# Attention scores and projections in plain fp32 on row tiles of the array, with pairs of PSUM banks

## The chip, the cores and the metric

The kernel runs on one core of a Trainium2 chip. The metric is the device time of one execution in microseconds (us). A core has a tensor engine (PE, which writes its results to the eight banks of PSUM), VectorE (DVE), ScalarE (ACT), GpSimd (POOL), a queue of DMA issues (SP) and 16 DMA engines. Every engine runs its instructions in the order in which the program issues them.

## What is computed

Eight batches of 512 tokens with 256 channels go through two layers. Each layer is an attention block and a feed-forward block, each added to its input, each behind a layer norm. Cut to what matters here:

```
def L0_attention(x, ctx):                 # x [8, 512, 256], ctx [8, 512, 128]; 16 heads of depth 16
    q, k, v = heads(x @ Wq + bq), heads(x @ Wk + bk), heads(x @ Wv + bv)
    att = where(causal, (q @ k.T) / 4, -inf)
    y = softmax(att) @ v
    qc, kc, vc = heads(x @ Wcq + bcq), heads(ctx @ Wck + bck), heads(ctx @ Wcv + bcv)
    y = y + softmax((qc @ kc.T) / 4) @ vc
    return y @ Wp + bp
def L1_attention(x, ctx):
    q, k, v = heads(x @ Wq + bq), heads(ctx @ Wk + bk), heads(ctx @ Wv + bv)
    return (softmax((q @ k.T) / 4) @ v) @ Wo + bo
x = x + L0_attention(layernorm(x), ctx)
x = x + L0_ffn(layernorm(x))              # weights and activations quantised
x = x + L1_attention(layernorm(x), ctx)
x = x + L1_ffn(layernorm(x))              # 8-bit steps with one scale per tensor
```

All inputs and outputs are fp32. The feed-forwards round to integers, so the attention in front of them has to be close to fp32.

## The kernel before

Attention is cut into units (kind, batch): S is the causal self attention, C the cross attention of layer 0, X that of layer 1. There are 8 of each, 24 in all, in the order `UNITS`: S and C of batches 0 to 5, then X units among the rest, and X units alone at the end. A unit has four groups of four heads, 96 groups in all.

**Operands.** A value is split in two float32r parts (a rounded form of fp32), its rounded high part and the rest; a product of two values is then three products of parts. The input of a projection is split so (`ln_job`, `ctx_job`), its weights too (`load_weight`; the parts are kept in DRAM and loaded again at each use). `prep_job` projects queries and keys of half of the heads, six matmuls per weight with 256 inputs and three with 128 (line 446), adds the bias on ScalarE (line 452) and splits the result on GpSimd (lines 238 and 255). `stack_job` copies the parts by DMA (lines 481 and 485) into the stack of a group, one of `NQK` = 4: 124 rows, so that one matmul over all of them gives the three products of parts, with zeros in K where another head's rows lie.

**Scores.** They are computed twice. `max_one` computes 128 queries of one head against up to 512 keys, one matmul into one bank (line 555), and VectorE takes the row maxima (line 565; for S with the causal mask added, line 560). `rows_job` negates the 16 columns of maxima (lines 576 and 577), turns them on PE (line 584) and writes them by DMA as four further rows of the stack, with ones in K, so that the second computation subtracts the maximum by itself. `exp_one` computes transposed scores, 128 keys against up to 512 queries, into one bank (line 627), adds the mask for S with a bf16 matmul (line 641), and ScalarE takes the exponential into a tile p (line 643). `av_part` multiplies by V in plain fp32, four heads side by side, each in its own 32 columns of the array (line 670); a column of ones in V gives the sums.

**After them.** `evac_job` copies the outputs to DRAM, `post_job` loads the sums, inverts them, loads them back spread over the heads' rows, multiplies (line 727) and splits again. `outproj_job` projects by `proj_tokens` (line 505, used for V too) and adds the residual. `last_heads_job` and `last_proj_job` do the same for the last unit in smaller pieces (lines 798, 813, 843, 852).

**The order of the work.** A planner (`Plan`) holds a rough clock for each engine. Jobs are generators that wait for due times on the tensor engine's clock; the main stream picks an output part first, then a step of maxima or one of exponentials, keeping the maxima `LEAD` steps ahead; work of jobs for PE gets its turn after the main stream had a share (`SHARE`). The program's order follows from these clocks, and on the chip each engine keeps to it. `CAPS` limits the PSUM banks: three for maxima, three for exponentials, two for outputs, three for work beside, out of eight.

**The end.** Behind the attention, the last feed-forward runs alone (from about 1495 us on); it is not changed.

## Time and profile before

| | |
|---|---|
| three runs | 1597.45, 1597.27, 1595.65 us; median 1597.27 |
| the profiled execution, span of its instructions | 1596.5 us |
| busy: PE, DVE, ACT, POOL | 94%, 81%, 68%, 52% |
| mean granted tensor clock | 0.981 |
| score matmuls, lines 555 and 627 | 1536 each |
| output matmuls, line 670 | 3072 records (two for each fp32 matmul) |
| row maxima, line 565 (128 x 512) | 1024 of 680 ns |
| exponentials, line 643 (128 x 512) | 1344 of 603 ns |
| bytes moved by DMA | 244.17 MB |

The profile page gives the busy time of each engine, groups of instructions by line, and the chain of work that ended last, followed back through what released each step. A matmul's length in it holds the drain of the array, which overlaps the next matmul; the distance between starts is what a stream of them costs. A stretch is a window of time with the busy time of each engine in it.

### The profile page before, as it was taken

The numbers are of one execution on the slowest core, as the hardware profiler recorded it, in microseconds if no ns is written. First come the engines' busy times: TensorE is split into PE (matmuls) and PEld (weight loads), VectorE is DVE, ScalarE is ACT, GpSimd is POOL, SyncE is SP. The second block draws the span as 40 slices with busy tenths as digits, with TensorE's granted clock in tenths as the row PEclk, the third lists the DMA queues.
The fourth block names the chain that finished last, engine by engine and source line by source line (L and its number), as shares of the span: only waits on it lengthen the run. The fifth ranks groups of instructions, "written<-read, shape, count | busy, mean of one in ns | idle before, by whom it ended". The sixth has DMA issues, their size and how long they took to land.

```text
span 1596.5 us, 28434 instructions
## 1 busy us (share of the span) xinstructions
PE 1500.6 (94%) x8911; PEld 905.9 (57%) x8928; DVE 1300.4 (81%) x3038; ACT 1087.0 (68%) x1934; POOL 832.8 (52%) x1059
## 2 busy tenths in 40 slices
PE   4989999999999999999999999999999989999876
PEld 3755665655665656655566465655555546555435
DVE  6878687887888888898869987888898768786687
ACT  3547667577676777677666767767776756777694
POOL 6543452653636745669447626456657434432328
PEclk8999999999999999999999999999999999999989
DMA  4664645755666646756467545755556564553422
GB/s 134 198 176 125 172 126 131 188 144 153 174 174 182 175 113 172 179 159 171 122 163 189 151 118 157 194 139 144 146 150 180 136 198 139 155 155 103 159 68 106
DMA packets 186110, 244.17 MB, mean 153 GB/s; under 512 B 82776, under 2 KB 92248, under 8 KB 185448
## 3 DMA queue, kind: packets, MB, share of 16 engines
q1 hardware_dynamic: 185960, 242.36, 56.6%
q8 instruction: 71, 1.16, 0.3%
q14 instruction: 79, 0.65, 0.1%
HBM read 101.18 MB, written 52.15 MB: 96 GB/s over the span
## 4 chain that ended last, share of the span: by engine, by line
PE 73%; DVE 11%; DMA 5%; ACT 4%; POOL 2%; issue 2%; SPq 1%; DVEq 0%; ACTq 0%; POOLq 0%
PE bank L670 18%; PE bank L555 18%; PE bank L627 17%; PE bank L446 6%; PE bank L505 5%; DVE mx L565 3%; ACT g L1414 2%; DMA qk<-qkt 2%; DVE bank L560 2%; PE bank L1063 2%; PE bank L641 2%; PE bank L381 2%; PE bank L1000 1%; DVE mhl L576 1%; ACT p L643 1%
## 5 line engine op out<-in xcount | busy, mean ns | idle before, releaser
L643 ACT ACTIVATE p<-bank 128x512 f32<-128x512 f32 x1344 | 737.5, 603 | 342.0 <-PE bank L627 221.9
L565 DVE TENSOR_REDUCE mx<-bank 128x1 f32<-128x512 f32 x1024 | 649.1, 680 | 120.7 <-PE bank L555 117.1
L555 PE MATMUL bank<-qk 124*128 124x512 f32 (+3 forms) x1536 | 552.4, 396 | 16.8 <-DMA scrz<-zr 7.3
L627 PE MATMUL bank<-qk 128*128 128x512 f32 (+3 forms) x1536 | 525.3, 387 | 11.9 <-DMA qk<-mrow 4.6
L555 PEld LDWEIGHTS bank<-qk 124*128 124x128 f32 x1536 | 283.7, 192 | 149.6 <-issue 69.6
L670 PE MATMUL bank<-p,v 128*32 128x512 f32 (+3 forms) x3072 | 365.4, 554 | 0.3
L627 PEld LDWEIGHTS bank<-qk 128*128 128x128 f32 x1536 | 282.2, 191 | 119.9 <-issue 42.2
L560 DVE CUSTOM_DVE_ANT_0 bank<-bank,mask 128x128 f32<-128x128 f32 (+3 forms) x512 | 238.4, 517 | 74.2 <-PE bank L555 71.9
L238 POOL TENSOR_SCALAR qkt<-qkt 128x512 fp32r<-128x512 f32 x92 | 57.0, 620 | 214.9 <-ACT qkt L452 145.2
L670 PEld LDWEIGHTS bank<-p,v 128*32 128x32 f32 x3072 | 66.6, 108 | 109.2 <-issue 81.3
L255 POOL TENSOR_TENSOR qkt<-qkt 128x512 fp32r<-128x512 f32 x92 | 118.3, 1286 | 7.7
L452 ACT ACTIVATE qkt<-bank,qk_bias 128x512 f32<-128x512 f32 x96 | 66.2, 689 | 37.0 <-PE bank L446 27.0
L641 PE MATMUL bank<-ident_b,mask_b 128*128 128x256 bf16 (+1 forms) x320 | 83.9, 262 | 0.0
L560 DVE DVE_READ_ACCUMULATOR2_ANT mx<- 128x1 f32 x512 | 71.9, 140 | 0.0
L727 POOL TENSOR_TENSOR oc<-oc,rb 128x512 f32<-128x512 f32 x31 | 39.7, 1282 | 60.7 <-DMA rb<-scrz 51.5
L243 ACT COPY ev<-bank 128x512 f32<-128x512 f32 x81 | 47.3, 583 | 19.8 <-PE bank L670 15.7
L1004 DVE SCALAR_TENSOR_TENSOR h<-bank,so,bc_l_b 128x512 f32<-128x512 f32 x64 | 47.2, 740 | 8.2 <-PE bank L1000 5.3
L641 PEld LDWEIGHTS <-mask_b 128*128 128x128 bf16 x320 | 30.7, 96 | 36.4 <-issue 26.2
L1482 PE MATMUL bank<-w2q,gq 128*128 128x256 bf16 x256 | 33.5, 295 | 13.2 <-POOL gq L259 6.5
L1414 ACT ACTIVATE g<-bank,b1s,sc_x 128x512 f32<-128x512 f32 x64 | 43.0, 971 | 2.5 <-POOL y L1396 2.5
L1413 PE MATMUL bank<-tyt,w1q 128*128 128x512 bf16 x127 | 37.6, 387 | 7.5 <-DVE tyt L1393 3.2
L761 POOL TENSOR_TENSOR xb<-xb,bc_l_bp 128x256 f32<-128x256 f32 x32 | 23.2, 739 | 38.9 <-DMA xb<-in_x 38.9
(264 smaller groups left out, 2059.8 us busy)
## 6 DMA issues: line engine op xcount, KB each, us to landing
qk<-qkt SPq DMA_DIRECT2D x288, 128.0 KB
qk<-qkt SPq DMA_DIRECT2D x576, 64.0 KB
scro<-ev SPq DMA_DIRECT2D x94, 256.0 KB
oc<-scro SPq DMA_DIRECT2D x47, 256.0 KB
rb<-scrz SPq DMA_DIRECT2D x47, 256.0 KB
x_d<-xb SPq DMA_DIRECT2D x15, 512.0 KB
xa_s<-in_x SPq DMA_DIRECT2D x8, 512.0 KB
xb<-in_x SPq DMA_DIRECT2D x8, 512.0 KB
```

What stands on the lines that cost most here:

```text
L255: nc.gpsimd.tensor_tensor(dst, full, high.bitcast(F32), ALU.subtract)
L446: nc.tensor.matmul(ps, wv[:, a, k, :], xs[:, e, k, :], start=(j == 0), stop=(j == len(seq) - 1))
L452: nc.scalar.activation(full, ps, AF.Identity, bias=bias)
L505: nc.tensor.matmul(ps[:, (t - t0) * C : (t - t0 + 1) * C], lhs[:, a, k, t * P : (t + 1) * P], wv[:, e, k, :], start=(j == 0), stop=(j == l ...
L555: nc.tensor.matmul(ps[:, :n], q[:, qt * P : (qt + 1) * P], k[:, :n], start=True, stop=True)
L560: nc.vector.tensor_tensor_reduce(out=ps[:, :n], in0=ps[:, :n], in1=mask[:, T - n :], scale=1.0, scalar=-3.0e38, op0=ALU.add, op1=ALU.max, ...
L565: nc.vector.tensor_reduce(dst, ps, AX.X, ALU.max)
L627: nc.tensor.matmul(ps[:, off : off + n], k[:, kt * P : (kt + 1) * P], q[:, q0:], start=off == 0, stop=kind != "S",)
L641: nc.tensor.matmul(diag, mask_b, ident_b.unsqueeze(1).broadcast_to([P, n, P]), start=False, stop=True)
L643: nc.scalar.activation(p, ps, AF.Exp, scale=0.25)
L670: nc.tensor.matmul(banks[av_t[G]][32 * j : 32 * j + 32, T - n :], v_t[un % 2][:, kt, h * VST : h * VST + 32], p, start=(i == 0), stop=last,)
L1414: nc.scalar.activation(g[:, f, b, :], ps, AF.Gelu, scale=sx[:, 2:3], bias=b1s[:, f : f + 1])
```

## The change

Scores, projections and their operands are plain fp32, with no split anywhere.

A group's operands are one tile of 128 rows, [row, (Q, K), 512], and there are six such tiles (`NQK` = 6). Each head has 32 rows, which is one row tile of the array: row 0 is for minus the maximum (ones in K, through the bias), rows 1 to 16 are the depth, the rest zeros. `prep_job` projects one group: weights are spread on the chip, once, to this layout (`spread`, in `weights_job`, which keeps all of them in SBUF), and the evacuation with the bias writes the operands directly. There is no `stack_job`.

A step of `max_one` or `exp_one` now covers two heads: one matmul for each, on two of the four row tiles, into the two banks of a pair. One reduction with negation (VectorE) or one exponential (ScalarE) then reads both banks. For S, steps of several sizes are packed, and both the maxima and the exponentials get their mask from bf16 matmuls on the whole array. Three pairs serve both uses; the last two banks are for outputs and for the work beside, one each (`CAPS`, `zone`).

The outputs stay in SBUF: sums go by DMA to a small tile, their inverses through DRAM into a tile of the outputs' layout, and GpSimd multiplies group by group. The output projection contracts four blocks of 128 rows (32 for each head, of which 16 carry values). The planner books a plain fp32 matmul of T columns as `2 * T` columns at 2400 per us (before: `4 * T`), a switch of the array's tiling with 0.08 us, and two lanes of row tiles that run side by side.

```diff
-NQK = 4  # operand stacks of four heads that are alive at once
-LEAD = 38  # steps that the maxima run ahead of the exponentials
+NQK = 6
+LEAD = 2.5
...
+MAXS = {"X": [(p, (qt,)) for qt in range(NT) for p in (1, 0)]}
+MAXS["S"] = [(p, qts) for qts in ((0, 2), (1,), (3,)) for p in (1, 0)]
+EXPS = {"X": [(p, (kt,)) for kt in range(NT) for p in (0, 1)]}
+EXPS["S"] = [(p, kts) for kts in ((0,), (1, 3), (2,)) for p in (0, 1)]
+AVS = {"X": [(0, 1), (2, 3)], "S": [(0,), (1, 2, 3)]}
...
-CAPS = {"sm": 3, "st": 3, "av": 2, "gn": 3}
+CAPS = {"sm": 2, "st": 2, "av": 1, "gn": 1}
+SWITCH = 0.08
...
-    def pe(self, cols, *deps):
-        return self.run("pe", 0.003 + cols / 2400, *deps)
+    def _pe_start(self, mode, *deps):
+        t = max(self.now, *(d + LAT for d in deps), 0.0)
+        if mode != self.mode:
+            t = max(t, *self.lane) + SWITCH
+            self.mode = mode
+        return t
+
+    def pe(self, cols, *deps, mode="full"):
+        t = max(self._pe_start(mode, *deps), *self.lane) + 0.003 + cols / 2400
+        self.clock["pe"] = t
+        self.lane = [t, t]
+        return t
+
+    def pe_rows(self, p, cols, *deps):
+
+        t = max(self._pe_start("rows", *deps), self.lane[p])
+        self.clock["pe"] = t + 0.02
+        self.lane[p] = t + cols / 2400 + 0.01
+        return self.lane[p] + 0.1
...
-    banks = [psum.tile([P, 512], F32, name=f"bank{i}") for i in range(8)]
+    pairs = [psum.tile([P, 2, T], F32, name=f"pair{i}") for i in range(4)]
+    banks = [pairs[i // 2][:, i % 2] for i in range(8)]
...
-    qk_t = [wp.tile([P, 3, 2, T], F32R, name=f"qk{i}") for i in range(NQK)]
+    qk_t = [wp.tile([P, 2, T], F32, name=f"qk{i}") for i in range(NQK)]
...
+    def spread(nm, u, raw, eng):
+
+        nk = WT[nm].shape[1]
+        for k in range(nk):
+            for h2 in range(2):
+                dst = WT[nm][:, k, 2 * u : 2 * u + 2].rearrange("p g (h c e) -> p g h c e", h=2, c=2)
+                src = raw[:, k * P : (k + 1) * P].rearrange("p (g c d h) -> p g h c d", g=2, c=2, h=2)
+                eng.tensor_copy(dst[:, :, h2, :, 1 : D + 1], src[:, :, h2])
...
-            seq = [(a, e, k) for a, e in PARTS for k in range(nk)]
-            for j, (a, e, k) in enumerate(seq):
-                if j % 2 == 0:
-                    yield pe_next()
-                nc.tensor.matmul(ps, wv[:, a, k, :], xs[:, e, k, :], start=(j == 0), stop=(j == len(seq) - 1))
-                tm = plan.pe(T)
...
+            for k in range(nk):
+                yield pe_next()
+                nc.tensor.matmul(ps, WT[nm][:, k, g], xs[:, k, :], start=(k == 0), stop=(k == nk - 1))
+                tm = plan.pe(2 * T)
             used(key, ring, tm)
...
+            t = evacuate(qk_t[G % NQK][:, i], ps, T, tm, bias=bias_of(nm, g))
...
-        ps = banks[pb]
-        nc.tensor.matmul(ps[:, :n], q[:, qt * P : (qt + 1) * P], k[:, :n], start=True, stop=True)
-        t = plan.pe(n)
...
+        ps = pairs[pb // 2]
+        size = [(qt + 1) * P if kind == "S" else T for qt in qts]
+        offs = [sum(size[:n]) for n in range(len(qts))]
+        for off, n, qt in zip(offs, size, qts):
+            for c in range(2):
+                rows = slice(32 * (2 * p + c), 32 * (2 * p + c) + 32)
+                q, k = qk_t[G % NQK][rows, 0], qk_t[G % NQK][rows, 1]
+                nc.tensor.matmul(
+                    ps[:, c, off : off + n], q[:, qt * P : (qt + 1) * P], k[:, :n],
+                    start=off == 0, stop=kind != "S",
+                )
+        t = plan.pe_rows(p, 2 * sum(size))
         if kind == "S":
-            nc.vector.tensor_tensor_reduce(
-                out=ps[:, :n], in0=ps[:, :n], in1=mask[:, T - n :], scale=1.0, scalar=-3.0e38,
-                op0=ALU.add, op1=ALU.max, accum_out=dst,
+
+            first, n = size[0] // P - 1, len(qts)
+            step = size[-1] // P if n == 2 else 1
+            for c in range(2):
+                diag = ps[:, c].rearrange("p (a b) -> p a b", b=P)[:, first : first + (n - 1) * step + 1 : step]
+                nc.tensor.matmul(diag, ident_b, mask_b.unsqueeze(1).broadcast_to([P, n, P]), start=False, stop=True)
+            t = plan.pe(2 * n * P)
+        for off, n, qt in zip(offs, size, qts):
+            nc.vector.tensor_reduce(
+                mx_t[G][:, 2 * p : 2 * p + 2, qt], ps[:, :, off : off + n], AX.X, ALU.max, negate=True
             )
-        else:
-            nc.vector.tensor_reduce(dst, ps, AX.X, ALU.max)
-        t = op("dve", n, t)
+            t = op("dve", 2 * n, t)
...
+            for c in range(2):
+                j = 2 * p + c
+                rows = slice(32 * j, 32 * j + 32)
+                q, k = qk_t[G % NQK][rows, 0], qk_t[G % NQK][rows, 1]
+                nc.tensor.matmul(
+                    ps[:, c, off : off + n], k[:, kt * P : (kt + 1) * P], q[:, q0:],
+                    start=off == 0, stop=kind != "S",
+                )
+                p_t[G, kt, j] = pt[:, c, off : off + n]
             off += n
...
+        t = plan.pe_rows(p, 2 * off)
...
+        nc.scalar.activation(pt[:, :, :off], ps[:, :, :off], AF.Exp, scale=0.25)
...
-            t = plan.pe(4 * n + 150)
+            t = plan.pe(2 * n + 60, mode="cols")
...
-                    acc[t // 2][0][:, (t % 2) * C : (t % 2 + 1) * C], yt[:, a, u, t * P : (t + 1) * P], wv[:, e, u, :],
-                    start=False, stop=(u, a) == (1, 1) and t % 2 == 1,
+                    acc[t // 2][0][:, (t % 2) * C : (t % 2 + 1) * C], y[:, g, t * P : (t + 1) * P], WT["Wo"][:, g],
+                    start=False, stop=g == 3 and t % 2 == 1,
```

## The prediction

> **What bounds the kernel now.** I read the page first (busy shares, the chain that ended last), then the stretches, then the tensor engine's own timeline, because a busy share alone does not say whether an engine streams or only has something in flight.
>
> ```profile
> PE 1500.6 (94%) x8911; PEld 905.9 (57%) x8928; DVE 1300.4 (81%) x3038; ACT 1087.0 (68%) x1934; POOL 832.8 (52%) x1059
> ...
> PE 73%; DVE 11%; DMA 5%; ACT 4%; POOL 2%; issue 2%; SPq 1%; DVEq 0%; ACTq 0%; POOLq 0%
> ```
>
> ```profile
> 100.00:1000.00 900.00, 875.55 (x5431) 535.40 (x5441) 751.45 (x1966) 624.54 (x1134) 480.78 (x612) 1.00 0.60 156
> ...
> 1300.00:1470.00 170.00, 166.39 (x905) 95.60 (x909) 132.38 (x256) 117.89 (x229) 72.35 (x102) 0.98 0.50 145
> ```
>
> The stretches (length; PE, PEld, DVE, ACT, POOL busy; granted clock) show PE busy for 97% in the causal part and in the last one, at full clock; VectorE stays at 83% and 78%. The chain agrees: 73% of it is PE. Is that streaming? The tensor engine's timeline (start, length, line, count) of one stretch:
>
> ```profile
> 701.73 0.40 PE L555 MATMUL bank<-qk 124*128 124x512 f32 x1
> 701.97 0.40 PE L627 MATMUL bank<-qk 128*128 128x512 f32 x1
> 702.21 0.40 PE L555 MATMUL bank<-qk 124*128 124x512 f32 x1
> 702.44 0.85 PE L627 MATMUL bank<-qk 128*128 128x512 f32 x3
> 703.13 0.40 PE L555 MATMUL bank<-qk 124*128 124x512 f32 x1
> 703.36 0.40 PE L627 MATMUL bank<-qk 128*128 128x512 f32 x1
> 703.60 0.40 PE L555 MATMUL bank<-qk 124*128 124x512 f32 x1
> 703.93 1.07 PE L670 MATMUL bank<-p,v 128*32 128x512 f32 x8
> 704.92 0.50 PE L627 MATMUL bank<-qk 128*128 128x512 f32 x1
> ```
>
> Read the starts, not the lengths. From 701.73 to 703.60 eight score matmuls start: 1.87/8 = 0.234 us per 512 columns of a float32r operand, back to back. So PE streams, and it bounds. The ninth line is one key tile's outputs, four heads side by side in column tiles, in plain fp32: eight records for four matmuls, 0.99 us to the next start. Between 703.60 + 0.23 and 703.93 lie 0.10 us for turning to column tiles. What a plain fp32 matmul costs on the whole array stands at the end of the last unit:
>
> ```profile
> 1480.64 1.05 PE L798 MATMUL bank<-ident_r,ol 128*128 128x128 f32 x8
> 1481.53 1.02 PE L843 MATMUL bank<-xb,ident_r 128*128 128x512 f32 x2
> 1482.39 0.83 PE L798 MATMUL bank<-ident_r,ol 128*128 128x128 f32 x6
> ```
>
> Line 843 issues one matmul per half and has two records: 1481.53 to 1482.39 is 0.86 us for 512 columns, 3.7 times the float32r one. Four 128-column ones (eight records) take 1480.64 to 1481.53: 0.22 each. The mean of a record, about 0.6 us, hides this; it must be counted per matmul.
>
> **The change part by part.** The profiled execution's span is 1596.5 us, 0.8 below the median of the runs (1597.27); I add to the span. Units: a "512" is one matmul of 512 columns. A cross group has 16 of them for maxima and 16 for exponentials, a causal group the equivalent of 10 + 10; 64 cross and 32 causal groups make 64 x 32 + 32 x 20 = 2688.
>
> *Scores.* Before: 2688 x 0.234 = 629 us. After, each is fp32 on 32 rows, 0.86, but a step issues two on different row tiles and the next step may use the other two. No row of this trace has row tiles; the nearest is the column tiling of line 670, where four fp32 matmuls of 512 end in 0.99 instead of 4 x 0.86, so I take side by side as working. A causal step is followed by mask matmuls on the whole array, so it never meets the next step: 20 / 2 x 0.86 x 32 = 275. A cross group has 16 steps: 8 slots if all go in pairs, 16 if none does. Only three pairs of banks are left, steps come one by one as a pair is released, and about ten pieces of other work per group (three projection pieces, two of outputs, one turned maximum, two of the output projection, one of values, one of the feed-forward) fall between; with evenly spread pieces about 6 of 16 gaps stay free, and not each has two different row tile pairs. I take 5 meetings, 11 slots: 11 x 0.86 x 64 = 605 (bounds 440 and 881). Together 880: +251.
>
> *Turning the array.* Each way 0.10 (from line 670). Causal: 12 steps, both ways, 24 x 0.10 x 32 = 77. Cross: about 6 runs of steps between other pieces, 12 x 0.10 x 64 = 77. +154, bounds 0 (hidden by loading ahead) and 308 (0.2 each). Line 670 is grouped into two bursts per group instead of four or three, and each costs 0.10 in and 0.13 beyond its streaming: 2 x 0.23 x 64 + 0.23 x 32 = -36.
>
> *Projections of queries and keys.* Before 480 float32r of 512 (six per weight with 256 inputs, three with 128, per two groups): 112 us. After 320 fp32 on the whole array: 128 causal, 192 cross; 320 x 0.86 = 275. +163. These have one place, PE, and no cover.
>
> *Values, output projection, transposes.* Line 505: 384 + 384 of 256 columns, three in 0.35 to 0.46 us, 0.135 each, 52 + 52. After: values 128 x 0.43 = 55 (+3), outputs 256 x 0.43 = 110 since each head's 16 rows are spread over 32 and the contraction takes four blocks instead of two (+58). Layer norm: 256 transposes at 0.10 against 128 at 0.22: +3. Transposed maxima: 96 x 0.12 = +12.
>
> *Masks.* 320 bf16 matmuls with 65,536 columns become 768 with 131,072, since the maxima's mask moves from VectorE to PE: at 0.11 per 256 columns (line 1063: four in 0.61 with their drain) +28.
>
> *What goes.* VectorE: 1024 reductions of 512 at 680 ns become 512 of 1024 (1205 ns, line 1023): 649 busy against about 617; causal 336 against 208 (two each of 256, 512, 768 and 1024 per group: 0.41, 0.68, 0.95, 1.21); lines 576 and 577, 69. It falls from 1300 to about 1070, plus a share of 192 bias evacuations of 0.69 instead of 96. ScalarE: 1344 exponentials at 603 ns become 704 steps of mostly 1.03: about 690 against 737. GpSimd loses the splits (118 + 57 on qkt alone) and divides the outputs by groups, 96 products and 32 sums of 1.28 = 164 us instead of 142 at lines 727 to 738, 255 and 238. SP loses 864 copies into the stacks, the round trip of the outputs and the reloads of weights, and gains one small copy per group each way. All this lies beside PE, the engine that is late, so I give it nothing but two things: waits for stack copies in the chain (32 us at 2%), of which I take 20 off, and a start without splits and copies (first masked maximum at 36.4 us now; four weight loads in turn then make about 24): -12. The end transposes two groups' outputs both ways in fp32: +5.
>
> Sum: 251 + 154 - 36 + 163 + 3 + 58 + 3 + 12 + 28 - 20 - 12 + 5 = 609; 1596.5 + 609 = 2205 us. Queues behind new waits: a score step waits on PE for a whole pair of banks, and projections and outputs queue behind it; a pair is held 0.86 + 0.17 (drain) + 1.1 + about 0.25 for signals = 2.4 us, 1408 steps / 3 x 2.4 = 1126 us, below PE's load, so it costs overlap, not time by itself. The one bank for side work is held likewise; its readers are idle more often than now.
>
> Two rules of the Trainium skill bear on this. "TensorE: Matmul & The Clock Gate" (Part 3, measured speedup) gives 3.07 times for four row tiles; by it all scores would cost 2688 x 0.86 / 3.07 = 753, and the sum would be 2078. "TensorEngine Tiling (Array Packing)" (Key Properties) says that a change of tiling mode drains the engine, which speaks against masks between row-tiled steps; it gives no price, and the row above has 0.10 each way.
>
> **The rivals.**
> *Faster.* fp32 is cheaper than I count. The changed planner books a whole-array fp32 matmul of T columns as 2 T at 2400 per us, 0.43 us. If that were so, and the steps met, scores would be 289, query and key projections 138, line 670's bursts half; PE would fall to some 1050, and VectorE (1070 plus evacuations) would bound: at its present 81% to 90% share, 1260 to 1400 us, say 1330. The terms that scale with the price are 880 + 275 + 55 + 110 = 1320; the change breaks even where these lose 609, at 0.46 us per 512. Against it: 0.86 at line 843 and 0.22 at line 798 in this trace.
> *The steps meet.* All cross steps in twos (-165) and turns hidden (-154): 1886; with some 95 us of present stalls gone too, because PE is always late, 1790. Still slower: even the bare streaming of the new work does not fit.
> *They don't.* No two steps meet: +276, 2481; with turns at 0.2, 2635. If row tiles did not run side by side at all, scores would be 2312 and the total 3637.
> *No change* would need gains of other engines to come onto the path by 609 us; 27% of the chain is not PE, 431 us, so it can't alone.
>
> **How the numbers follow.** My case, partial meeting, 1820 to 2550: 0.80. Better than 1820 but slower than now: 0.06. Over 2550: 0.08. Faster: 0.04. Within 0.2%, about what a measurement of this kernel can tell from no change: 0.02. The time is that of the likeliest case, 2205; the range is its bounds drawn in a little at the top (2635) and below (1790), 1820 to 2550. Slower by over 0.2% is 0.80 + 0.06 + 0.08 = 0.94.
>
> **What would show it.** PE over 90% busy with VectorE and ScalarE near 50%; starts of fp32 projections 0.86 apart; score records of 512 about 0.6 long with four row tiles' starts close together in some places and two in others; a gap near 0.1 at each mask; a chain of over 75% PE. Wrong would be: projections 0.43 apart, VectorE above 85%, or PE idle before scores for lack of banks.

## The result and the profile after

The changed kernel takes 2599.79 us (median of 4 runs, 2592.41 to 2610.25) against 1597.36 for the kernel before (4 runs beside it): 1.6262 times as long, 95% interval 1.6196 to 1.6327. The prediction was 2205 with a range of 1820 to 2550. The direction was right, the size 395 us short, and the time lies 50 us above the range.

The page of the changed kernel: the span, the busy time of each engine, the granted clock in 40 slices, the first line of the chain of waits.

```profile
span 2608.5 us, 31907 instructions
...
PE 2370.8 (91%) x12669; PEld 932.6 (36%) x12712; DVE 1228.7 (47%) x1656; ACT 1049.3 (40%) x1243; POOL 587.9 (23%) x833
...
PEclk9999899899999899999998999998998898969857
...
PE 25%; ACT 3%; DVE 2%; issue 1%; DMA 1%; POOL 1%; SPq 0%; another core or an unknown queue 0%; DVEq 0%; ACTq 0%; POOLq 0%
```

PE is over 90% busy, VectorE and ScalarE fall below half: as predicted. Two things are not. The clock row, 9 almost everywhere before, has 8s throughout and falls to 5 at the end. And the chain covers only a third of the span (25% PE, 9% others), so that it says little here; the stretches and the tensor engine's timeline have to be read instead. The stretches (start:end, length, busy time of PE, PEld, DVE, ACT and POOL, granted clock, share of DMA, GB/s):

```profile
200.00:1000.00 800.00, 764.02 (x4290) 299.07 (x4302) 364.70 (x501) 299.81 (x358) 165.88 (x216) 0.95 0.11 32
...
2000.00:2300.00 300.00, 260.15 (x1257) 95.77 (x1264) 140.66 (x214) 134.95 (x153) 86.59 (x132) 0.90 0.17 50
2300.00:2500.00 200.00, 147.64 (x651) 62.61 (x649) 75.19 (x99) 68.59 (x88) 28.83 (x43) 0.79 0.19 64
```

From 200 to 1000 us PE has something in flight for 95.5% of the time, at a clock of 0.95; towards the end it is idle for up to a quarter, at 0.79. Now the tensor engine's timeline (start, length, line, count of records) of one piece:

```profile
2199.52 1.12 PE L489 MATMUL pair<-cxt_X,w_Xk 128*128 128x512 f32 x2
2200.58 1.13 PE L551 MATMUL pair<-qk 32*128 32x512 f32 x4
2201.64 1.12 PE L489 MATMUL pair<-xlt_x,w_Xq 128*128 128x512 f32 x2
2202.69 1.13 PE L551 MATMUL pair<-qk 32*128 32x512 f32 x4
2203.75 1.13 PE L489 MATMUL pair<-xlt_x,w_Xq 128*128 128x512 f32 x2
2204.80 1.14 PE L551 MATMUL pair<-qk 32*128 32x512 f32 x8
2205.88 1.12 PE L489 MATMUL pair<-cxt_X,w_Xk 128*128 128x512 f32 x2
```

Each line is one stretch of one tiling. A step of two heads (four records) takes 1.06 us from start to start, two steps side by side (eight records) 1.08, a whole-array matmul 1.05 to 1.06. A plain fp32 matmul of 512 columns streams 0.86; so about 0.20 is lost at every change, not 0.10.

To see where 1012 us of span came from I added up, from the starts of all records of the tensor engine, when at least one matmul streams (two clocks a column for each of an fp32 matmul's two records, 0.234 us per 512 of float32r, one clock for bf16) and what the gaps are. In a half-speed stretch streaming takes twice as long, and the half of it is put down as extra. Gaps under 0.005 us are left out, so the columns fall short of the span from the first to the last matmul by some 5 us.

| us | before | after | more | the prediction's terms |
|---|---|---|---|---|
| streaming | 1270 | 1892 | +622 | +523 |
| gaps up to 0.3, at a change of tiling or in the first matmul behind it | 125 | 291 | +166 | +118 |
| other gaps up to 0.3 | 67 | 15 | -51 | 0 |
| gaps over 0.3 (waits) | 95 | 275 | +179 | -32 |
| half speed | 18 | 119 | +101 | 0 |

(The terms: streaming 251 + 163 + 3 + 58 + 3 + 12 + 28 + 5; changes 154 - 36; waits -20 - 12.) Which of the short gaps belong to a change depends a little on where the line is drawn; the two rows together are +115. The five differences add up to 1017. Of the 408 us that the sum 609 lacks, 312 are waits and half speed (179 + 32 and 101), which the prediction did not have at all. By where they stand, 28 us of the waits are before scores (lines 551 and 616), 71 before outputs (line 660), 77 before projections, output projection and transposes, 57 in the last feed-forward (lines 1372 and 1441), and the rest elsewhere. The experiments go to the prices first, then to the order, then to the clock, and last to the waits, where the largest cause was found.

### The profile page after: what moved, and what is told of

It is laid out like the page before. It is cut to its first block, busy times and chain, and to the rows that moved or that the text cites. A ratio compares the mean times of both kernels' runs of the same rounds, so it can differ in the third digit from the quotient of the medians.

```text
span 2608.5 us, 31907 instructions
## 1 busy us (share of the span) xinstructions
PE 2370.8 (91%) x12669; PEld 932.6 (36%) x12712; DVE 1228.7 (47%) x1656; ACT 1049.3 (40%) x1243; POOL 587.9 (23%) x833
## 5 line engine op out<-in xcount | busy, mean ns | idle before, releaser
L565 DVE TENSOR_REDUCE mx<-pair 128x2 f32<-128x1024 f32 (+3 forms) x768 | 823.1, 1090 | 913.1 <-PE pair L551 547.0
L633 ACT ACTIVATE p<-pair 128x1024 f32<-128x1024 f32 (+1 forms) x704 | 682.3, 985 | 957.8 <-PE pair L616 483.4
L616 PE MATMUL pair<-qk 32*128 32x512 f32 (+3 forms) x3072 | 711.9, 589 | 14.3 <-ACT p L633 8.1
L551 PE MATMUL pair<-qk 32*128 32x512 f32 (+3 forms) x3072 | 709.4, 596 | 3.4 <-DVE mx L565 1.3
L660 PE MATMUL pair<-p,v 128*32 128x512 f32 (+3 forms) x3072 | 338.1, 558 | 59.2 <-DVE h L980 18.3
L616 PEld LDWEIGHTS pair<-qk 32*128 32x128 f32 x3072 | 244.5, 190 | 302.2 <-issue 191.3
L551 PEld LDWEIGHTS pair<-qk 32*128 32x128 f32 x3072 | 222.7, 189 | 271.8 <-issue 200.9
L716 POOL TENSOR_TENSOR y<-ev,rb 128x512 f32<-128x512 f32 x62 | 78.5, 1267 | 513.3 <-DMA rb<-scrz 513.3
L290 ACT ACTIVATE qk<-pair,qk_bias 128x512 f32<-128x512 f32 x137 | 94.1, 687 | 239.1 <-PE pair L489 237.1
L660 PEld LDWEIGHTS pair<-p,v 128*32 128x32 f32 x3072 | 81.6, 111 | 266.1 <-issue 140.0
L489 PE MATMUL pair<-xlt_x,w_Xq 128*128 128x512 f32 x128 | 74.3, 684 | 7.5 <-ACT ev L288 3.1
L746 PE MATMUL pair<-w_Wp,y 128*128 128x256 f32 x256 | 77.9, 431 | 3.2 <-ACT ev L288 3.2
```

The costliest lines, as they stand in the source:

```text
L290: nc.scalar.activation(dst, src, AF.Identity, bias=bias)
L489: nc.tensor.matmul(ps, WT[nm][:, k, g], xs[:, k, :], start=(k == 0), stop=(k == nk - 1))
L551: nc.tensor.matmul(ps[:, c, off : off + n], q[:, qt * P : (qt + 1) * P], k[:, :n], start=off == 0, stop=kind != "S",)
L565: nc.vector.tensor_reduce(mx_t[G][:, 2 * p : 2 * p + 2, qt], ps[:, :, off : off + n], AX.X, ALU.max, negate=True)
L616: nc.tensor.matmul(ps[:, c, off : off + n], k[:, kt * P : (kt + 1) * P], q[:, q0:], start=off == 0, stop=kind != "S",)
L633: nc.scalar.activation(pt[:, :, :off], ps[:, :, :off], AF.Exp, scale=0.25)
```

## The experiments

All versions beside each other; the last five columns are worked out as above from each profiled execution (here the short gaps hold those under 0.005 us too), the time is the median.

| | time | streaming | gaps up to 0.3 | waits | half speed | changes of tiling |
|---|---|---|---|---|---|---|
| before | 1597 | 1270 | 198 | 95 | 18 | 792 |
| the changed kernel | 2600 | 1892 | 311 | 275 | 119 | 1862 |
| cross steps in twos (e2) | 2498 | 1786 | 300 | 279 | 109 | 1775 |
| pieces kept together (e3) | 2478 | 1884 | 262 | 253 | 60 | 1635 |
| no masks (e4) | 2501 | 1796 | 244 | 345 | 96 | 1418 |
| e2 and e3 (e6) | 2461 | 1806 | 275 | 273 | 102 | 1649 |
| true prices (e7) | 2513 | 1912 | 297 | 228 | 63 | 1780 |
| e2, e3 and e7 (e8) | 2420 | 1804 | 277 | 260 | 75 | 1615 |
| four side banks, with e7 (e10) | 2827 | 1880 | 322 | 364 | 252 | 1767 |
| float32r scores (e5) | 2142 | 1215 | 320 | 439 | 156 | 1862 |
| and projections (e11) | 2140 | 1017 | 316 | 478 | 319 | 1844 |
| e11 with e2, e3 and e7 (e12) | 2119 | 984 | 275 | 532 | 316 | 1633 |
| own banks (e14) | 2403 | 1894 | 323 | 138 | 31 | 1862 |
| own banks and e8 (e15) | 2261 | 1800 | 298 | 125 | 26 | 1615 |
| own banks and e12 (e16) | 1898 | 986 | 306 | 347 | 241 | 1633 |

### The prices by themselves (e1)

```diff
+    # two row tiles, then the whole array; likewise each form again and again, and float32r
+    for i in range(35):
+        rows(qk, i % 2, i % 2)
+        full(w, qk[:, 0])
```

> A kernel of matmuls alone, in eight stretches, with nothing else running; it leaves out the whole computation and writes zeros. It measures the disputed prices by themselves. Stretches: 512-column fp32 on the whole array; fp32 on the same two row tiles; fp32 on four row tiles; two row tiles and the whole array in turn; two row tiles and two masks in turn; float32r on four row tiles; float32r row tiles and whole array in turn; float32r on the whole array. Theory 'turning' (what was mis-sized is the change of tiling, 0.2 us and not 0.1): whole array 0.86 us a matmul, two row tiles 0.86 a step, four row tiles 0.86 for both steps, row tiles and whole array in turn 1.06 + 1.06 a round, with masks about 1.06 + 0.3. With 0.1 a change the rounds would be 0.2 shorter. Theory 'clock' (half-filled rows of the array count as little work, and the granted clock falls to half): the stretch on two row tiles shows a granted clock near 0.5 after some us and a step near 1.7; the one on four tiles stays at 1.0. If the clock has another cause, both stay at 1.0. float32r on four row tiles should be near 0.23 for both steps if it keeps its price of the whole array.

Two row tiles again and again took 60.28 us for 70 steps, 0.861 each; four row tiles 60.30 for 70 pairs of steps, again 0.861; the whole array 0.866. So side by side is free to the full: four matmuls on four row tiles in the time of one on the whole array. ("TensorE: Matmul & The Clock Gate", Part 3, measured speedup, has 3.07 times for four row tiles; here 4 x 0.866 / 0.861 is 4.0, and the measurement decides.) Alternating forms cost:

```profile
232.31 1.13 PE L97 MATMUL pair<-qk 32*128 32x512 f32 x4
233.36 1.12 PE L100 MATMUL pair<-qk,w 128*128 128x512 f32 x2
234.42 1.13 PE L97 MATMUL pair<-qk 32*128 32x512 f32 x4
235.48 1.12 PE L100 MATMUL pair<-qk,w 128*128 128x512 f32 x2
```

1.05 to 1.06 us to each next start, with nothing to wait for: 0.20 per change, the same as in the kernel. In the kernel's records it has two parts: a gap at the change (168 us in 1735 gaps, 0.097 each) and a second one between the two records of the first fp32 matmul behind it (0.10 on row tiles, 0.107 on the whole array). Behind a change to the outputs' column tiles, and to the masks, the second one is nearly nothing (about 0.01). A step with two bf16 masks behind it took 1.27 us a round. ("TensorEngine Tiling (Array Packing)", Key Properties, says that a change of mode drains the engine. A gap at every change fits that; whether the engine drains to the end the runs do not show. They give the price that the page leaves open.)

Two row tiles alone, half of the array's rows, ran at full clock for all of their stretch. The stretch of float32r row tiles and whole array in turn did not, though nothing in it waits; after 10 us it fell to half speed and stayed there (busy times as above, the granted clock is the number behind POOL's):

```profile
69.00:128.00 59.00, 59.00 (x278) 26.40 (x276) 0.00 (x0) 0.00 (x0) 1.00 0.00 1
475.00:485.00 10.00, 10.00 (x36) 4.33 (x36) 0.00 (x0) 0.00 (x0) 1.00 0.00 0
485.00:556.00 71.00, 71.00 (x147) 28.34 (x147) 0.00 (x0) 0.00 (x0) 0.50 0.00 0
```

About half of that stretch's time is gaps at the changes, and half of what streams fills half of the array.

### The order: steps in twos, pieces together, no masks, true prices (e2, e3, e4, e6, e7, e8)

e2 lets a cross step start only if two pairs are free, and issues two:

```diff
-        t = plan.bank_at("sm")
+        two = i % 2 == 0 and UNITS[G // 4][0] != "S"
+        t = plan.two_at("sm") if two else plan.bank_at("sm")
```

> The changed kernel, with the steps of cross groups issued in twos (all four row tiles) once two pairs of banks can be had. The profile of the change has about 640 slots for the 1024 cross steps (10.0 of 16, the prediction took 11) and 436 runs of them. 'Turning' and 'clock': slots go to 512, 128 x 0.86 = 110 us less, half-clock time before the last feed-forward falls from 248 us to under 100, some 75 us less, runs fall a little; about 2400 us. 'Waits' (three pairs of banks are the limit, and PE idles for them, 238 us against 96 before): two pairs at once are had later, VectorE and ScalarE drain both together, and PE idles more; 2600 us or above.

2498.25 us, ratio 1.5607 (1.5553 to 1.5660). Streaming falls by 106 us, waits (279) stay, and there are only 87 changes fewer: the gain is that of the fuller slots. Half speed falls by 10 us only, where 75 were expected.

e3 takes the planner's turn points out of the middle of projections, values, output projection and feed-forward pieces:

```diff
-            for k in range(nk):
-                yield pe_next()
+            yield pe_next()
+            for k in range(nk):
                 nc.tensor.matmul(ps, WT[nm][:, k, g], xs[:, k, :], start=(k == 0), stop=(k == nk - 1))
```

> The changed kernel, with the whole-array work of the jobs left in larger pieces (both halves of a projection, four matmuls of values, eight of the output projection, eight of the feed-forward): about 300 fewer pieces, the same matmuls. 'Turning' at 0.2: if each of 300 stood alone between steps, two changes less each, 120 us less; since some already follow each other, 60 to 100 less, about 2520 us. With 0.1 a change half of it. 'Waits': nothing by the turning, at most a few us by shorter holds of the one bank for side work; 2580 to 2610.

2477.67 us, ratio 1.5526 (1.5448 to 1.5604). 227 changes fewer took 49 us of short gaps with them (0.2 each), and 59 us of half speed and 22 of waits went too.

e4 leaves out the mask matmuls (lines 562 and 631), so that the causal part is unmasked:

```diff
-                nc.tensor.matmul(diag, ident_b, mask_b.unsqueeze(1).broadcast_to([P, n, P]), start=False, stop=True)
```

> The changed kernel without the mask matmuls of causal units, so causal scores are not masked and that part of the computation is left out. 'Turning' at 0.2: 768 changes less, 154 us, and 768 matmuls of 131,072 bf16 columns, 55 us; causal steps can meet, up to 137 of their 275 us, say 70: about 2330 us. At 0.1 a change and no meeting: 77 + 55, about 2470 us. 'Waits': with the masks gone PE waits for the same pairs instead, under 60 us less, 2540 us or above.

2501.32 us, ratio 1.5656 (1.5583 to 1.5729). 444 changes and 96 us of streaming go, 163 us with the gaps, but 70 us come back as waits. The time lies between the cases expected: without the masks PE waits for something else. What, this run does not show.

e6 puts e2 and e3 together, e7 only mends the planner's prices, e8 is all three:

```diff
-SWITCH = 0.08
+SWITCH = 0.2
...
-                tm = plan.pe(2 * T)
+                tm = plan.pe(4 * T)
```

> Both edits together: cross steps issued in twos, and whole-array pieces kept together. Alone they gave 2498 (-102) and 2478 (-122). If each acts by its own term (streaming of half-filled slots; number of changes and clock) they add: 2376. If both only moved the same half-clock time, they do not add: 2450 to 2480. If waits grow, since longer pieces hold the only bank for side work while two pairs are wanted at once: 2500 or more.

> The changed kernel, with only its planner's book prices altered to the measured ones: a plain fp32 matmul 4 clocks a column instead of 2, a change of tiling 0.20 us instead of 0.08. The instructions are the same, only their order can differ. Theory that PE's waits (196 us) and the half clock come of an order planned for a PE that is twice as fast: waits fall by about half, and changes by some 10%, as the planner sees what they cost: 2430 to 2500. Theory that the order is set by the released banks and by how few there are, not by the prices: within 2% of the changed kernel, 2550 to 2650.

> All three edits of order: true prices, cross steps in twos, pieces kept together. What is left must be paid: streaming of about 876 + 632 + 308 = 1816 us, and some 1550 changes at 0.20 = 310; so 2130 is a floor without any wait or half clock, and 2300 to 2400 if waits and clock stay as in the runs with single edits. Under 2300 would say that the waits came from the planner's wrong prices; over 2400 that the edits get in each other's way.

2461.44 (1.5387, 1.5323 to 1.5450), 2513.39 (1.5711, 1.5675 to 1.5746) and 2419.93 (1.5105, 1.5067 to 1.5144). e2 and e3 do not add, and e8 came out above the 2300 to 2400 expected of it. True prices take 47 us off the waits and 56 off the half speed, but in none of these do waits fall below 228. Order is worth 180 us in all; most of PE's waits do not come from it.

### Plain fp32 against float32r (e5, e11, e12)

```diff
-    qk_t = [wp.tile([P, 2, T], F32, name=f"qk{i}") for i in range(NQK)]
+    qk_t = [wp.tile([P, 2, T], F32R, name=f"qk{i}") for i in range(NQK)]
```

> The changed kernel, only that queries, keys and the transposed maxima are kept as float32r, so that a score of 512 columns on 32 rows streams once instead of twice; the order of the work and the masks are unchanged, so the number of changes of tiling is about the same (1862). Price theory: the rows' streaming falls from 993 us by the ratio measured side by side (0.229 against 0.861), to 264: 729 less, 1871 us if nothing else moves, and PE's turnings (372 us), now beside less streaming, become the largest single loss. Waits theory: the three pairs of banks, held about 2.4 - 0.65 = 1.75 us each, 1408 / 3 x 1.75 = 820 us, and ScalarE (1049) and VectorE (1229) come up to PE; waits take back 100 to 300 of it: 1970 to 2170. Clock theory: as the share of time that streams falls towards a half, as in the alternating float32r stretch, the clock falls to a half in long stretches: PE's remaining 930 us of streaming cost up to half as much again, 2100 to 2300. No theory lets it come under the kernel before (1597).

2142.07 us, ratio 1.3384 (1.3357 to 1.3411): of 677 us of streaming 458 come through, and 164 come back as waits, 37 as half speed. The time lies in the ranges of both the waits and the clock theory; by the table it is more the waits. So the price of plain fp32 in the scores is under half of the 1002 us that the change costs; the rest of the plain fp32 work, the changes of tiling, the waits and the half speed cost the other part.

> Queries and keys in float32r (2142), and now their projections too, 320 matmuls of 512 columns on float32r operands; the context is rounded by one more copy on GpSimd for each batch and kind. Values, outputs and the output projection stay plain fp32. Price theory: 320 x (0.86 - 0.23) = 202 less streaming: 1940. If PE's waits and clock take back as they did with the scores (458 of 729 came through): 126 less, 2016. If PE is no longer what binds: 2100 or more.

2139.60 us, ratio 1.3388 (1.3311 to 1.3465): 198 us of streaming less, and no gain at all. The expectations asked which engine binds instead, but by the profile no engine does: what PE streams less is lost again at half speed. The stretch from 200 to 1000 us with float32r scores alone:

```profile
200.00:1000.00 800.00, 717.27 (x4120) 298.32 (x4118) 472.21 (x647) 393.03 (x476) 212.69 (x284) 0.94 0.14 41
```

and with float32r projections too:

```profile
200.00:1000.00 800.00, 701.84 (x3932) 300.27 (x3928) 456.50 (x632) 392.00 (x486) 225.16 (x307) 0.81 0.15 41
```

PE does less and is granted 0.81 instead of 0.94. The half-speed extra doubles from 156 to 319 us and waits grow by 39: 202 us, which take back all of the 198.

> The same, with the three edits of order (true prices, cross steps in twos, pieces kept together), which took 180 us off the plain fp32 version. If they take as much here: about 1830. The kernel before (1597) is reached only if the turnings, waits and half-speed stretches that are left (some 370 + 320 + 210 us in the float32r run) fall to half together, which no run so far speaks for; if it stays above 1900, waits for banks and not order set the time.

2119.39 us, ratio 1.3258 (1.3210 to 1.3306). The three edits of order, worth 180 us in fp32, are worth 20 here, with 316 us of half speed.

### What sets the clock (e9, e13)

In every profile the granted clock changes at whole multiples of 3.41 us from one phase. For the changed kernel and its seven plain fp32 variants (e2, e3, e4, e6, e7, e8, e10) I took each window of 3.41 us at full speed, and what the next one was. Twice: by the share of the time that PE streams, and by that share times the share of the array that is filled (a row tile fills 32 of 128 rows).

| share in the window | by time alone: windows, of these followed by half speed | by time x fill: windows, of these followed by half speed |
|---|---|---|
| under 0.30 | 59, 38 | 117, 96 |
| 0.30 to 0.35 | 29, 19 | 80, 50 |
| 0.35 to 0.40 | 35, 19 | 163, 40 |
| 0.40 to 0.50 | 98, 45 | 623, 0 |
| 0.50 to 0.60 | 197, 30 | 1209, 0 |
| over 0.60 | 4769, 35 | 2995, 0 |

Time alone does not separate them; time x fill does: of 4827 windows above 0.40 none was followed by half speed, and between 0.30 and 0.40 it is mixed. The way back is as sharp: of half-speed windows under 0.7 by time x fill, 513 of 519 were followed by another, above 0.8 only 2 of 144. At half speed a column takes twice the time, so 0.75 there is about 0.37 in columns, in the middle of the mixed zone. It follows that a piece of work of half-filled steps alone cannot get back, whatever it waits for: it reaches 0.5 at most. The fill differs in these windows by rows alone, since the outputs' column tiles run four side by side. That was only a count over runs; two runs set it up.

```diff
+    def paced(n, m, k):
+        for i in range(n):
+            for _ in range(m):
+                full()
+            nc.vector.tensor_copy(t1[:, :k], pairs[3][:, 0, :k])
```

> Leaves out the whole computation; it measures what a wait does to the clock. Plain fp32 matmuls of 512 columns on the whole array, with waits for VectorE between them, no change of tiling at all. In the profile of the changed kernel the clock is granted for stretches of 3.4 us, and a stretch at half speed follows one in which PE streamed little: of the full-speed stretches with 30 to 40% streaming 7 in 10 were followed by half speed, with 40 to 50% 4 in 10, with over 60% hardly any. Duty theory: three matmuls between waits (about 72% streaming) and two (63%) run at full speed, one with a wait of 1 us (46%) falls to half for most of its time, one with a short wait (65%) stays full; a single wait of about 0.9 us costs itself, one of about 4.8 us costs itself and at least one stretch at half speed, 1.7 us or more on top. Rival: the halves come of changes of tiling or of half-filled arrays, then nothing here falls below full speed.

On the whole array no paced wait lowered the clock, one matmul and a wait (0.45) included, which the expectation had at half speed: it went by time in the kernel's windows, without the fill. The rival is not right either, since a long wait did lower it. A single wait of 0.78 or 2.23 us cost itself alone. A wait of 5.13 us was followed by 6.8 us at half speed, each of three times; here is one:

```profile
507.02 1.02 PE L92 MATMUL pair<-qk,w 128*128 128x512 f32 x2
513.17 2.08 PE L92 MATMUL pair<-qk,w 128*128 128x512 f32 x2 [5.13 <-DVE t L123]
515.04 28.07 PE L105 MATMUL pair<-qk,w 128*128 128x512 f32 x60
```

In this one the matmul behind the wait takes 1.87 us to the next start instead of 0.96, and 30 matmuls 28.07 instead of 25.91: 3 us on top of 5.13 (2 to 3 us in the three cases).

```diff
+    def step(lane):
+        for c in range(2):
+            r = slice(32 * (2 * lane + c), 32 * (2 * lane + c) + 32)
+            nc.tensor.matmul(pairs[lane][:, c], qk[r, 0, :P], qk[r, 1], start=True, stop=True)
```

> Leaves out the whole computation. The same waits for VectorE as before (a period is m x 0.864 + 1.04 us), once after whole-array matmuls, once after steps of two row tiles (half of the array's rows), once after four row tiles side by side; each stretch 40 to 95 us, with whole-array streaming in between. Fill theory: what decides is the share of time that PE streams times the share of the array that it fills, with the step to half speed somewhere between 0.33 and 0.40: whole array two and a wait 0.62 full; two row tiles two and a wait 0.31 half; four row tiles, two slots and a wait 0.62 full; two row tiles four and a wait 0.38 in between; two row tiles six and a wait 0.41 full; one whole-array matmul and a wait 0.45 full; one step of two row tiles and a wait 0.22 half; one slot of four row tiles and a wait 0.45 full. Rival, streaming time alone: two row tiles behave as the whole array with the same count, all of them full.

The eight stretches in that order (whole array two; two row tiles two; four row tiles two slots; two row tiles four; two row tiles six; whole array one; two row tiles one; four row tiles one slot); the granted clock is the number behind POOL's:

```profile
34.00:115.00 81.00, 58.27 (x119) 20.02 (x118) 20.09 (x30) 0.00 (x0) 1.00 0.00 0
148.00:274.00 126.00, 104.57 (x223) 32.50 (x220) 18.90 (x28) 0.00 (x0) 0.50 0.00 0
304.00:384.00 80.00, 57.57 (x464) 20.95 (x464) 19.87 (x29) 0.00 (x0) 1.00 0.00 1
424.00:560.00 136.00, 122.53 (x274) 43.01 (x272) 11.74 (x17) 0.00 (x0) 0.50 0.00 0
598.00:752.00 154.00, 143.69 (x328) 52.49 (x324) 8.98 (x13) 0.00 (x0) 0.50 0.00 0
781.00:855.00 74.00, 43.42 (x79) 11.68 (x79) 26.95 (x39) 0.00 (x0) 1.00 0.00 0
888.00:992.00 104.00, 75.44 (x148) 18.09 (x144) 24.87 (x36) 0.00 (x0) 0.50 0.00 0
1021.00:1096.00 75.00, 44.76 (x313) 12.48 (x314) 27.04 (x40) 0.00 (x0) 1.00 0.00 1
```

With the same waits, half-filled steps fall to half speed and stay there, whole-array matmuls and full slots of four row tiles do not. Streaming time alone is refuted. Six steps and a wait, 0.41 on the average, fell too: a window that holds a whole wait of 1.04 us has (3.41 - 1.04) / 3.41 x 0.5 = 0.35, and once is enough, since there is no way back.

"TensorE: Matmul & The Clock Gate" (Part 1, and "HAM oscillation") describes such windows of 3.41 us and gives the rule "no PE-idle gaps >~3.4µs". The windows agree. On the whole array these runs do not speak against the rule: a gap of 2.23 us did nothing, one of 5.13 us lowered the clock. With half the array filled it is not enough: gaps of 1 us lowered the clock too, so what counts besides time is the fill.

### Are the side banks too few? (e10)

```diff
-CAPS = {"sm": 2, "st": 2, "av": 1, "gn": 1}
+CAPS = {"sm": 2, "st": 2, "av": 1, "gn": 3}
...
-        self.zone = {6, 7}
+        self.zone = {4, 5, 6, 7}
```

> The changed kernel with the true prices in its planner (2513), and two pairs of banks for scores with four banks for outputs and side work, instead of three pairs and two. Theory that PE's waits are the side work's, whose pieces share one bank: outputs, projections, output projection and transposes wait 94 of 163 us there; these fall by more than half, and the half-speed stretches that follow them too: 2400 to 2450. Theory that the pairs bind as soon as there are two: a pair is held about 2.4 us for 1408 steps, 1408 / 2 x 2.4 = 1690, still under the span, but steps find a free pair later and fewer go side by side: up to 6 slots of 0.86 more in each of 64 cross groups, 330: 2600 to 2850.

2827.40 us, ratio 1.7667 (1.7587 to 1.7748), against 2513 with three pairs. The waits moved, as both theories say in their parts: those before outputs fell from 51 to 24 us, those before scores rose from 20 to 227. But not for fewer steps side by side: streaming fell by 32. What PE waits for most (engine, line, releaser: us in total, times, longest):

```profile
PE pair L616 <- ACT p L633: 88.7, 104, 1.9
PE pair L551 <- ACT p L633: 66.6, 66, 1.2
```

and 252 us of half speed behind them. The side work still had halves of pairs here. So banks matter on both sides; it is not enough to move them.

### Waits on the other half of a pair (e14, e15, e16)

What held PE showed in the last feed-forward, which the change does not touch. The tensor engine's timeline there, before:

```profile
1499.51 40.52 PE L1413 MATMUL bank<-tyt,w1q 128*128 128x512 bf16 x125 [0.22 <-issue]
```

and after, of some thirty such lines:

```profile
2470.08 1.86 PE L1372 MATMUL pair<-tyt,w1q 128*128 128x512 bf16 x4 [1.38 <-ACT g L1373]
2472.81 1.86 PE L1372 MATMUL pair<-tyt,w1q 128*128 128x512 bf16 x4 [0.87 <-ACT g L1373]
2475.55 1.87 PE L1372 MATMUL pair<-tyt,w1q 128*128 128x512 bf16 x4 [0.87 <-ACT g L1373]
```

The same matmuls, once in one run of 40.52 us, once in groups of four with a wait for ScalarE each, at half speed, 85 us (2467.6 to 2553.1). Six banks go round in both. But in the change a bank is one half of a tile `pair`, and what writes to a tile waits for those who read it: the upper half of a pair waits until ScalarE has read the lower one, which was written a moment ago. In the instructions as they are built, 402 of the 554 waits of PE on readers of the fourth pair, whose halves are the banks of outputs and side work, name a reader of the other half, and so do all 32 of line 1372 on readers of its tile. By this count the two banks work as little more than one. The experiment makes them tiles of their own, and all eight banks in the last feed-forward:

```diff
-    pairs = [psum.tile([P, 2, T], F32, name=f"pair{i}") for i in range(4)]
-    banks = [pairs[i // 2][:, i % 2] for i in range(8)]
+    pairs = [psum.tile([P, 2, T], F32, name=f"pair{i}") for i in range(3)]
+    banks = [pairs[i // 2][:, i % 2] for i in range(6)] + [psum.tile([P, T], F32, name=f"bank{i}") for i in (6, 7)]
...
+    psum_stack.close()
+    psum = ctx.enter_context(tc.tile_pool(name="psum_tail", bufs=1, space=PSUM))
+    banks[:] = [psum.tile([P, T], F32, name=f"tbank{i}") for i in range(8)]
```

> The changed kernel, only that the banks which are used singly are tiles of their own: banks 6 and 7 (outputs and side work) during the attention, all eight in the last feed-forward. In the changed kernel they are halves of a pair's tile, and the program that it builds makes a write to one half wait for the reader of the other: 402 of the 554 waits that PE has for readers of the fourth pair's tile name an instruction that reads the other bank. Theory that these waits are the ones PE stands in: in the last feed-forward PE and ScalarE go in turns (1.87 and 0.87 us), which goes, and the stretch falls from 143 us to the 102 of before: -40; in the attention, of the 71 us before outputs (line 660) and the 77 before projections, output projection and transposes more than half goes: -80; the half-speed stretches that follow waits fall with them, about 50 of 100 us: -50; together 2430. Theory that the two banks are simply too few, so that the true waits stand right behind the false ones: only the last stretch gains, 2540 to 2570.

2402.76 us (6 runs, 2399.76 to 2407.43), ratio 1.5026 (1.4991 to 1.5060): 197 us less than the changed kernel, with the same instructions in the same order on PE. Streaming, changes and short gaps are as before; waits are halved from 275 to 138, half speed falls from 119 to 31. What PE waits for in the changed kernel:

```profile
PE pair L1372 <- ACT g L1373: 29.0, 32, 1.6
...
PE pair L660 <- DVE h L980: 18.3, 12, 2.1
PE pair L660 <- ACT qk L290: 13.7, 17, 1.2
```

and with own banks:

```profile
PE bank L746 <- POOL y L716: 27.5, 4, 14.2
PE bank L660 <- DVE h L980: 8.6, 5, 2.1
```

The line of the last feed-forward in its timeline:

```profile
2301.97 40.70 PE L1375 MATMUL tbank<-tyt,w1q 128*128 128x512 bf16 x125 [0.22 <-issue]
```

PE runs through again, in 40.70 us, and the stretch takes 108 us (from 2290 on) instead of 144. In the attention the waits before outputs, 71 us by the gaps, are 29. The stretch from 200 to 1000 us ran at a clock of 1.00 instead of 0.95.

> Own banks and the three edits of order (true prices, cross steps in twos, pieces kept together; without own banks 2420). Waits in the attention were 198 us there, 101 of them before outputs. If own banks take as much off as in the theory above: 2420 - 40 - 80 - 30 = 2270. If the true waits stand behind the false ones: 2380.

2260.54 us, ratio 1.4140 (1.4102 to 1.4179), expected 2270. Own banks (197) and the edits of order (180) add nearly: 2223 by their sum.

> Own banks, the edits of order, and float32r in scores and in the projections of queries and keys (2119 without own banks, with 532 us of waits over 0.3 us and 316 of half speed). If the false waits feed the half speed: less than 150 us of half speed and 300 of waits, 1750 to 1850. If half-filled steps with true waits are enough for the half speed: 1950 or more. Under 1597 nothing expects it: streaming (984), changes (275), ends and the last stretch leave 1400 with no wait at all.

1898.03 us, ratio 1.1872 (1.1841 to 1.1902): 221 less than without own banks, but 347 us of waits and 241 of half speed stay. The time lies between the two ranges; the waits and the half speed speak for the second theory. 223 us of these waits stand before scores (lines 572 and 638), where every step writes both banks of a pair and its reader reads both, so they are true waits (92 us for ScalarE's exponentials, 57 for VectorE's maxima among those that the profile names): with steps of 0.23 us PE waits for the pairs, and half-filled steps with waits are the work that falls to half speed. No version came under the kernel before.

## Why the prediction was wrong, point by point

*Right.* PE is the busiest engine before and after, and VectorE and ScalarE end at 47% and 40%. A plain fp32 matmul of 512 costs 0.86 on the whole array (0.866) and on row tiles, and two steps side by side cost one (0.861 for both); with that the faster rival, which needed 0.46, falls. (Its 289 us of scores let causal steps meet too, which the prediction itself rules out; it would be 357, and nothing hangs on it.) The sign "a chain of over 75% PE" did not come, since the chain covers a third of the span.

*Scores.* Predicted 880 us of slots, measured 946 us of streaming. With 273 for the causal part, 673 are left for 64 cross groups: 12.3 slots of 0.854 instead of 11. Mechanism right, size 66 us short; many steps meet only in part. (The 10.0 in the expectation of e2 counts runs of steps that overlap at all; 12.3 is their time in slots.) All other streaming was short by 33.

*Turning the array.* "Each way 0.10 (from line 670)" was the gap at the change alone, and that it is, 0.097. A second gap of the same size follows inside the first fp32 matmul on row tiles or on the whole array behind it, 0.10 to 0.107. The prediction's row of outputs (0.99 instead of 0.86) does not hold it: that is the gap of 0.10 on the way out and little more. It stood one row further, where a float32r matmul that streams 0.23 takes 0.34 to the next start:

```profile
704.92 0.50 PE L627 MATMUL bank<-qk 128*128 128x512 f32 x1
705.26 0.63 PE L555 MATMUL bank<-qk 124*128 124x512 f32 x2
```

The term came out 48 us short; 51 us of other short gaps, which the float32r stream had and the change removed, were not in the sum and cancel it.

*The waits: 20 and 12 us taken off, nothing added.* This is the step that failed. Waits rose by 179, where the prediction took 32 off. The prediction worked out how long a pair of banks is held for a step, found 1126 us against a longer PE, and concluded that this "costs overlap, not time by itself". For the pairs that held: 28 us of waits stand before scores. It named "PE idle before scores for lack of banks" as a sign of being wrong, and the waits came before outputs and side work instead. It did not ask the same of the two banks that are not pairs, though it wrote that the one bank for side work "is held likewise", and it took halves of a tile for banks. The diff showed the line (`banks = [pairs[i // 2][:, i % 2] ...]`). Tiles of their own, with the same instructions in the same order on PE, took away 137 us of the waits, 88 of the half speed, and 197 of the time. Of the last feed-forward the prediction said nothing, as it is not changed; it took some 40 us longer.

*The clock.* Not a term. 119 us of half speed against 18. It follows waits, as e14 shows, and half-filled steps, as e13 shows: the prediction's own layout of two heads on two of four row tiles halves the fill. How much of the 119 us each of the two makes is not shown: in e2, with fewer half-filled slots, it stayed at 109.

*The range.* Its upper end came from "they don't meet" and turns at 0.20 (2635), pulled in to 2550. It had no rival in which waits grow, and waits and half speed are 312 us of what is missing.

With own banks the kernel takes 2403 us, 198 above the prediction. By the table 101 of that are streaming (624 more than before, against 523), 7 short gaps (125 against 118), 75 waits (43 more than before, where the prediction took 32 off) and 13 half speed.

What stays open: why waits fall by a sixth with true prices, with the same tiles; how much of the 0.30 to 0.40 zone of the clock is a matter of where the windows lie; and what would take away the remaining waits of e16.

## What to carry to other kernels

A bank that is used singly should be a tile of its own: what makes two banks one tile for an instruction that reads both also makes a write to one wait for the reader of the other, and the profile shows it as two engines going in turns where a ring should let them overlap. Price a change of array tiling from start to start of a whole alternation, not from one gap, and count all stretches, not only those of the new work. Where steps fill half of the array, a short wait costs more than itself, since the clock goes by streaming time times fill in windows of 3.41 us; work taken off PE then comes back as half speed (e11: 198 us less streaming, no gain that can be told from noise).

## What was not expected of the hardware

- The granted clock fell to 0.5 after windows of 3.41 us in which streaming time times the filled share of the array was low: after most of those below 0.35, after some from 0.35 to 0.40, after none of the 4827 above 0.40. At half speed it mostly came back where this product was above 0.8 and mostly stayed where it was under 0.7; at half speed 0.75 of the time is about the number of columns of 0.37 at full speed. Half-filled steps with a wait of 1.04 us after every six stayed at 0.50 for all of a stretch of 154 us.
- Four row tiles cost the same as two: 0.861 us per slot for four fp32 matmuls of 512 columns, and 0.866 for one on the whole array.
- A change of tiling between row tiles and the whole array costs 0.20 us in plain fp32, half of it at the change and half between the two records of the first matmul behind it. To column tiles and to bf16 masks the second half is nearly nothing (about 0.01).
